# Transposes of x and x1 by VectorE and DMA in a four-layer graph attention kernel

## The chip, the cores and the metric

The kernel runs on one core of one Trainium2 chip. The core has five engines with queues of their own: TensorE (PE; its weight loads are shown as PEld), VectorE (DVE), ScalarE (ACT), GpSimd (POOL) and SyncE (SP), which here issues nearly all DMAs. The metric is the device time of the core in microseconds, the median of several runs; lower is better.

## The reference

16 samples x of 1024 nodes and 128 features pass through three transformer layers whose attention is masked by one adjacency matrix, and then through a graph attention layer:

```python
# layers 0 to 2, 8 heads of 16
scores = einsum('bnhd,bmhd->bhnm', h @ Wq, h @ Wk) / sqrt(16)
attn = softmax(where(adj == 0, -inf, scores))
x = layer_norm(h + (einsum('bhnm,bmhd->bnhd', attn, h @ Wv) @ Wo + bo), ln1_g, ln1_b)
x = layer_norm(x + relu(x @ W1 + b1) @ W2 + b2, ln2_g, ln2_b)
# layer 3
h = x @ W
e = leaky_relu((h @ a_src)[:, :, None] + (h @ a_dst)[:, None, :], 0.2)
out = layer_norm(softmax(where(adj == 0, -inf, e)) @ h + x, ln_gamma, ln_beta)
```

## The kernel before, in words

The work is cut into 48 **blocks**, one per sample and layer, in the order of `blocks` (line 655): four samples go through layer 0, then the same four through layers 1 and 2, then the next four. A block has 32 **steps**: two groups of four heads (g), two query halves (qh) and eight key tiles (kt). In a step (`score_step`, line 415) PE computes the scores of two pairs of heads, each into one of three PSUM buffers `s`; then each 128x1024 tile is masked and passed through exp in one of two ways. On DVE, a mask of zero or a large negative number is added while the tile is read from PSUM (L433), and ACT takes exp in place (L445). On POOL, ACT takes exp straight from PSUM (L430) and POOL multiplies by a mask of ones and zeros (L431). The second pair always goes through DVE; the first goes through POOL except in the steps named by `BOTH_ON_DVE`. Four steps later (`AHEAD`) `av_step` (line 447) multiplies by the values on PE and accumulates in `acc`, so PE, in its order, reaches the value matmul of a step behind the scores of the fourth step after it.

All other work is cut into **pieces**, at most one of them put behind a step by `piece` (line 691), in the order of a list of chains. Pieces of the kinds `proj` and `post` have a due step in the table `AT`; those of the last layer have a gap to the piece ahead of them. A chain that is due but stands behind another waits for a later step. For a block m:

- `proj_tasks(m)` (line 357) runs during block m-1: `t0` transposes x by halves on PE against an identity (`transpose_half`, line 281, instructions L286) and ACT copies it out of PSUM (L289, or L291 with the scale and shift of the norm before it); `split` projects to queries and keys and splits them into a high and a low part (L385 on ACT, L386 on DVE); `v` projects the values. Then `stack` (line 401) lays the parts out over partitions by 16 DMAs of 128 KB per head group (L408), the first group at step 21, the second at step 1 of the block itself.
- `post_tasks` (line 469) runs during block m+1: `gather` transposes the attention output on DVE (L477), `out_proj` projects it, DVE adds x (L329) and takes statistics (L322, L324), POOL normalises (`normalise`, L337 to L341), `x1t` transposes x1 on PE as above, POOL applies scale and shift (`scale_shift`, L345, L346), and `ffn1` and `ffn2` follow; after `ffn2` POOL normalises again, half by half.
- `last_tasks` (line 541) computes the last layer of a sample behind its third `post`: transposes, node values, rows g and h spread by 16 small DMAs, then four times `edges` and `aggregate`, and `end`, which stores the result.

The order of PE and ACT in the loop is as written; that of DVE, POOL and SP is settled by the scheduler when the kernel is built.[...]

Of the kernel before, what the change touches and what calls it, by code (L numbers as in the profile page):

```python
# [18 lines left out]
P = 128  # L19
# [4 lines left out]
SLOT = 32  # L24
# [9 lines left out]
AT = {"proj": (3, 6, 9, 11, 14, 17, 19, 20), "post": (12, 22, 23, 25, 26, 27, 28, 30, 32, 40, 41)}  # L34
AT_END = {3: (12, 21, 22, 24, 25, 26, 27, 28, 30, 31), 2: (8, 9, 13, 14, 15, 16, 17, 18, 20, 21)}
AHEAD = 4
BOTH_ON_DVE = (2, 5, 7)
TILES = {"w": 10, "x": LANES + 1, "last": 2}
# [77 lines left out]
def fast_path(ctx: ExitStack, tc: tile.TileContext, a: dict, out: bass.AP, flag):  # L116
# [32 lines left out]

    def load_x(b):  # L150
        t = work.tile([P, NT, D], F32, tag="x", name="x", bufs=TILES["x"])
        nc.sync.dma_start(t, x_dram[b].rearrange("(t p) d -> p t d", p=P))
        return t
# [115 lines left out]

    v_bufs = []  # L270
# [10 lines left out]
    def transpose_half(name, src, h, gain=None, bias=None):  # L281

        dst = half_tile(name)
        ps = bank()
        for t in range(4):
            nc.tensor.transpose(ps[:, t * P:(t + 1) * P], src[:, 4 * h + t, :], identf)  # L286
        with soon():
            if gain is None:
                nc.scalar.copy(dst, ps)  # L289
            else:  # L290
                nc.scalar.activation(dst, ps, AF.Identity, scale=gain, bias=bias)  # L291
        return dst

    def by_columns(dst, lhsT, rhs, start=True, stop=True):

        for j in range(0, P, SLOT):
            nc.tensor.matmul(dst[j:j + SLOT, :], lhsT[:, j:j + SLOT], rhs, start=start, stop=stop)  # L297
# [7 lines left out]
    def project(lhs, rhs, h, out):  # L305

        ps = bank()
        for t in range(4):
            for f in range(len(lhs)):
                by_columns(ps[:, t * P:(t + 1) * P], lhs[f][:, t * P:(t + 1) * P], rhs[f],  # L310
                           start=(f == 0), stop=(f == len(lhs) - 1))
# [45 lines left out]
    def proj_tasks(m):  # L357
        b, l = blocks[m]
        w = W[l]
        s = {}  # L360

        def t0(h):
            def run():
                x = state["x", b]
                if l == 0:
                    s["xT", h] = transpose_half("xT", x, h)
                    if h == 1:
                        nc.gpsimd.tensor_add(x, x, rows(w["bo"]))
                else:

                    s["xT", h] = transpose_half("xT", x, h, W[l - 1]["ln2_gc"], W[l - 1]["ln2_bc"])
                    if h == 1:
                        scale_shift(x, W[l - 1]["ln2_g"], w["bo"])
            return run

        def split(n, h):
            def run():
# [5 lines left out]
                by_columns(ps, w[n], s["xT", h])  # L383
                with soon():
                    nc.scalar.copy(hi[:, c], ps)  # L385
                    nc.vector.tensor_sub(lo[:, c], ps, hi[:, c].bitcast(F32))  # L386
            return run

        def v(h):
# [4 lines left out]
            return lambda: project([s["xT", h]], [w["Wv"]], h, out)  # L394

        pieces = [t0(0), t0(1), split("Wk", 0), split("Wk", 1), split("Wq", 0), split("Wq", 1), v(0), v(1)]
        return [(2 if n in (3, 4, 5, 6) else 1, f, {0: "+w", 1: "+w", 6: "-w", 7: "-w"}.get(n, "")) for n, f in enumerate(pieces)]
# [17 lines left out]
    def score_step(step):  # L415
# [3 lines left out]
        for pp in range(2):  # L419
# [7 lines left out]
            on_pool = pp == 0 and kt not in BOTH_ON_DVE  # L427
# [4 lines left out]
            else:  # L432
                behind["dve"] = nc.vector.tensor_add(ev, psv, m).ins  # L433
                masked.append((2 * step_no[0] + pp + (kt not in BOTH_ON_DVE), ev))
# [34 lines left out]
    def post_tasks(b, l):  # L469
# [20 lines left out]
        def x1t(h, alone=False):  # L490
            def run():
                x1 = s["n1"][0]
                s["x1T", h] = transpose_half("x1T", x1, h, w["ln1_gc"], w["ln1_bc"])
                if alone:
                    scale_shift(x1[:, 4 * h:4 * h + 4, :], w["ln1_g"], w["b2"])
                elif h == 1:
# [3 lines left out]
        def ffn1(f, h):  # L500
            def run():
                s["h", f, h] = half_tile("hT")
                ps = bank()
                by_columns(ps, w["W1"][:, f * P:(f + 1) * P], s["x1T", h])
# [4 lines left out]
        def ffn2(h):  # L509
            def run():  # L510
# [4 lines left out]
                normalise(s["n2"], slice(4 * h, 4 * h + 4))  # L515
# [7 lines left out]
        together = [(5, both, "+w +w"), (1, out_proj(0), "-w"), (1, out_proj(1), "-w"), (5, x1t(0), "+w"), (1, x1t(1), "+w")]  # L523
        for h in range(2):
            together += [(1, ffn1(0, h), "+w"), (1, ffn1(1, h), "+w -w")]
        together += [(1, ffn2(0), "-w -w"), (1, ffn2(1), "-w -w")]
        alone = [[(1, gather(h), "+w"), (1, out_proj(h), "-w"), (3, x1t(h, True), "+w"), (1, ffn1(0, h), "+w"),
                  (1, ffn1(1, h), "+w -w"), (1, ffn2(h), "-w -w")] for h in range(2)]
# [12 lines left out]
    def last_tasks(b):  # L541
# [3 lines left out]
        def xt(h):  # L545
            def run():
# [6 lines left out]
                s["xT", h] = transpose_half("xT", state["x", b], h, w["ln2_gc"], w["ln2_bc"])  # L553
# [44 lines left out]
        def edges(u):  # L598
            def run():
                e = s["e", u] = e_tile().rearrange("p j (c q) -> p (j c) q", q=256)  # L600
                for c in range(2):

                    ps = slot()
                    for i in range(2):
                        for r in range(2):
# [3 lines left out]
                                             g_rows[row, u * 256:(u + 1) * 256], start=True, stop=True)  # L609
                    nc.vector.scalar_tensor_tensor(e[:, c:NT:2, :], ps.rearrange("p (j q) -> p j q", q=256), 1.0,  # L610
                                                   mask01[:, c:NT:2, u * 256:(u + 1) * 256], op0=OP.max, op1=OP.mult)
            return run

        def aggregate(u):
            def run():
                e, ps = s["e", u], bank()
                for i in range(2):
                    for t in range(NT):
                        by_columns(ps[:, i * (D + 1):(i + 1) * (D + 1)], e[:, t, i * P:(i + 1) * P],
# [14 lines left out]
        def end():  # L634
            y = s["n"][0]
            for h in range(2):
                scale_shift(y[:, 4 * h:4 * h + 4, :], wl["ln_gamma"], wl["ln_beta"])
                queue = nc.scalar if h and b == B - 1 else nc.sync
                queue.dma_start(out[b].rearrange("(t p) d -> p t d", p=P)[:, 4 * h:4 * h + 4], y[:, 4 * h:4 * h + 4, :])
# [62 lines left out]
    with tc.manual_schedule(engines={mybir.EngineType.PE, mybir.EngineType.Activation, mybir.EngineType.DVE,  # L702
                                     mybir.EngineType.SP}):
        load_rows(range(4))
        put(proj_tasks(0), ("proj", 0))
# [21 lines left out]
    def av_due(n):  # L727

        for item in [w for w in waiting if w[2] <= n]:
# [24 lines left out]
            elif g == G - 1 and qh == 1:  # L754
                post = post_tasks(b, l)[0]
# [296 lines left out]
```

## Time and profile before

| | |
|---|---|
| median of 3 runs | 3985.54 us (3984.45 to 3985.72) |
| profiled execution | 3983.09 us |
| its span, first to last instruction | 3981.2 us |
| mean granted clock of TensorE | 0.987 |
| PE busy | 3758.5 us (94%) |
| DVE busy | 3408.3 us (86%) |
| ACT busy | 3392.8 us (85%) |
| POOL busy | 3331.4 us (84%) |
| share of the 16 DMA engines, SP's queue | 22.5% |

Durations below are those of the profiled execution, in us unless marked ns. An L number is a line of the kernel. Neighbouring instructions of DVE and ACT overlap by some 0.1 us, so that busy time is less than the count times the mean[...].

### The profile page before, as it was taken

How to read it: one execution, taken by the hardware profiler on the slowest of the kernel's cores; microseconds unless marked ns; L12 is line 12 of the kernel's file. 1: busy time of each engine (PE TensorE's matmuls, PEld its weight loads, DVE VectorE, ACT ScalarE, POOL GpSimd, SP SyncE). 2: the span in 40 equal slices, each digit the busy share in tenths (PEclk: the TensorE clock that was granted, in tenths of full speed). 3: DMA queues.
4: the chain of work that ended last, by engine and by line, in shares of the span. 5: the costliest groups of instructions: out<-in, count | busy, mean ns of one | idle time of the engine just before them, and what ended most of it. 6: DMA issues, size and time to landing. Idle time of an engine off the chain costs nothing.

```text
span 3981.2 us, 107823 instructions
## 1 busy us (share of the span) xinstructions
PE 3758.5 (94%) x44501; PEld 1558.5 (39%) x44501; DVE 3408.3 (86%) x5326; ACT 3392.8 (85%) x3961; POOL 3331.4 (84%) x3010
## 2 busy tenths in 40 slices
PE   7999999999999999999999999999999999999996
PEld 2333333344443333334444333333444433333345
DVE  7888988988888988988888898888888898898874
ACT  7999999977779999997777999999777799999860
POOL 4788888987789888988778888888877898898875
PEclk8999999999999999999999999999999999999998
DMA  6222222112222222222222222221222212222200
GB/s 163 65 65 53 55 65 63 46 48 65 56 58 57 65 65 54 54 65 55 55 55 55 65 53 56 65 64 45 55 55 55 71 46 62 65 51 58 66 8 20
DMA packets 124465, 233.13 MB, mean 59 GB/s; under 512 B 34624, under 2 KB 73792, under 8 KB 123968
## 3 DMA queue, kind: packets, MB, share of 16 engines
q1 hardware_dynamic: 123056, 225.74, 22.5%
q8 instruction: 354, 5.80, 0.6%
q14 instruction: 143, 1.17, 0.1%
q10 hardware_dynamic: 912, 0.42, 0.0%
HBM read 15.54 MB, written 8.39 MB: 6 GB/s over the span
## 4 chain that ended last, share of the span: by engine, by line
PE 61%; DVE 22%; POOL 9%; ACT 4%; issue 3%; SPq 0%; DMA 0%; DVEq 0%; ACTq 0%; POOLq 0%
PE acc L450 23%; PE t L297 19%; PE s L423 16%; DVE e L433 13%; POOL e L431 3%; POOL x L341 2%; PE t L286 2%; DVE lo L386 2%; DVE st L322 2%; ACT e L445 2%; ACT e L430 2%; DVE tt L461 1%; POOL mv L339 1%; PE s L297 1%; POOL x L345 1%
## 5 line engine op out<-in xcount | busy, mean ns | idle before, releaser
L433 DVE TENSOR_TENSOR e<-s,mask_add 128x1024 f32<-128x1024 f32 x2112 | 2493.6, 1213 | 344.6 <-PE s L423 263.7
L445 ACT ACTIVATE e<-e 128x1024 f32<-128x1024 f32 x2112 | 2203.4, 1060 | 206.1 <-DVE e L433 187.9
L431 POOL TENSOR_TENSOR e<-e,mask 128x1024 f32<-128x1024 f32 x960 | 1933.5, 2026 | 419.0 <-ACT e L430 419.0
L450 PE MATMUL acc<-e,v 128*17 128x512 f32 x12288 | 1627.8, 601 | 73.3 <-DVE tt L461 47.8
L423 PE MATMUL s<-Wq,Wk 64*128 64x512 f32 x6144 | 1185.0, 456 | 58.1 <-DVE e L433 41.3
L430 ACT ACTIVATE e<-s 128x1024 f32<-128x1024 f32 x960 | 980.8, 1022 | 227.5 <-PE s L423 226.5
L423 PEld LDWEIGHTS s<-Wq,Wk 64*128 64x128 f32 x6144 | 501.2, 185 | 1027.9 <-DVE e L433 417.1
L450 PEld LDWEIGHTS acc<-e,v 128*17 128x17 f32 x12288 | 208.6, 95 | 582.1 <-issue 452.0
L341 POOL TENSOR_SCALAR x<-x,mv 128x128 f32<-128x128 f32 x896 | 389.1, 447 | 23.5
L345 POOL TENSOR_TENSOR x<-x,ln_g 128x1024 f32<-128x1024 f32 (+1 forms) x97 | 229.5, 2367 | 25.1 <-PE t L286 22.6
L339 POOL TENSOR_TENSOR mv<-mv,half_neg 128x4 f32<-128x4 f32 x224 | 232.4, 1038 | 18.6
L297 PE MATMUL t<-hd,e 128*32 128x129 f32 x7040 | 208.2, 275 | 1.2
L329 DVE TENSOR_TENSOR x<-t,x 128x512 f32<-128x512 f32 x191 | 130.8, 685 | 86.9 <-PE t L297 86.9
L297 PEld LDWEIGHTS t<-hd,e 128*32 128x32 f32 x7040 | 194.6, 110 | 16.0 <-issue 5.0
L322 DVE BATCH_NORM_STATS2 st<-x 128x6 f32<-128x128 f32 x896 | 197.3, 280 | 3.3
L297 PE MATMUL t<-x1T,W 128*32 128x512 f32 x1520 | 198.0, 592 | 0.0
L297 PEld LDWEIGHTS t<-W,hT 128*32 128x32 f32 x6080 | 170.0, 110 | 58.5 <-issue 45.5
L297 PE MATMUL t<-W,hT 128*32 128x128 f32 x6080 | 183.4, 273 | 0.2 <-DVE x L625 0.2
L286 PE MATMUL t<-identf,x 128*128 128x128 f32 x872 | 151.0, 289 | 34.0 <-DVE lo L386 15.4
L286 PEld LDWEIGHTS t<-identf,x 128*128 128x128 f32 x872 | 92.9, 141 | 230.2 <-issue 108.3
L337 POOL TENSOR_SCALAR mv<-mv 128x4 f32<-128x4 f32 x224 | 53.0, 236 | 124.6 <-DVE mv L324 98.8
L610 DVE SCALAR_TENSOR_TENSOR e<-s,mask 128x1024 f32<-128x1024 f32 x128 | 150.3, 1214 | 5.9 <-PE s L607 5.0
(118 smaller groups left out, 2573.9 us busy)
## 6 DMA issues: line engine op xcount, KB each, us to landing
Wk<-hi SPq DMA_DIRECT2D x384, 128.0 KB
Wk<-lo SPq DMA_DIRECT2D x384, 128.0 KB
Wq<-hi SPq DMA_DIRECT2D x384, 128.0 KB
Wq<-lo SPq DMA_DIRECT2D x384, 128.0 KB
x<-in_x_dram SPq DMA_DIRECT2D x16, 512.0 KB
out_dram<-x SPq DMA_DIRECT2D x31, 256.0 KB
ai<-in_adj_dram SPq DMA_DIRECT2D x8, 512.0 KB
g_rows<-parts SPq DMA_DIRECT2D x124, 4.0 KB
```

The lines of the kernel that those rows point to most:

```text
L286: nc.tensor.transpose(ps[:, t * P:(t + 1) * P], src[:, 4 * h + t, :], identf)
L297: nc.tensor.matmul(dst[j:j + SLOT, :], lhsT[:, j:j + SLOT], rhs, start=start, stop=stop)
L322: nc.vector.bn_stats(st[:, t, :], z[:, t, :])
L339: nc.gpsimd.tensor_tensor(v, v, half_neg[:, ts], OP.pow)
L341: nc.gpsimd.tensor_scalar(z[:, t, :], z[:, t, :], mv[:, t, 0:1], mv[:, t, 1:2], op0=OP.add, op1=OP.mult)
L345: nc.gpsimd.tensor_mul(z, z, rows(gain, n))
L423: nc.tensor.matmul(ps[:, r * 512:(r + 1) * 512], k[64 * r:64 * r + 64, kt * P:(kt + 1) * P], q[64 * r:64 * r + 64, q0:q0 + 512], start=Tru ...
L430: nc.scalar.activation(ev, psv, AF.Exp, scale=HD ** -0.5)
L431: behind["pool"] = nc.gpsimd.tensor_mul(ev, ev, m).ins
L433: behind["dve"] = nc.vector.tensor_add(ev, psv, m).ins
L445: nc.scalar.activation(ev, ev, AF.Exp, scale=HD ** -0.5)
L450: nc.tensor.matmul(acc[j * SLOT:j * SLOT + HD + 1, :], v_bufs[m % 2][:, kt, 2 * j + g, :], e[:, j, :], start=first, stop=last)
```

## The change

1. **x and x1 are transposed without PE.** `transpose_by_dma`: two DVE instructions transpose a sample's tile in 32x32 blocks into a buffer `xb` (one buffer), and 16 DMAs on SP, of 32 KB each, carry the blocks to their partitions in `xT` or `x1T`. For this a sample's tokens are laid out in another order (`tokens`), so x is loaded by eight DMAs and the result stored by eight, and the last layer reads its mask and edge rows in strided form: four DVE instructions of 256 columns for one of 1024. PE still transposes x of the first block, x1 of the last two blocks and the input of the last layer.
2. **The call.** x for block m+2 is transposed at step 25 of block m, if it is ready; x1 is one piece, called with the table's step 17 ahead of `ffn1` at 24. Before it was a piece per half.
3. **Norm scale and shift** are folded into W1, b1, Wq, Wk, Wv and bo once, at step 40 (`fold_norms`). Queries and keys then have a bias of their own from layer 1 on, added in the instructions of `split`.
4. **Tables.** The due steps of all pieces, the steps in which both tiles are masked on DVE (11 of 32, not 12), the first stack at step 23, eight buffers `w` instead of ten, two buffers `xt` of a whole sample.
5. After `ffn2` POOL normalises all eight tiles at once, not four and four.

```diff
-AT = {"proj": (3, 6, 9, 11, 14, 17, 19, 20), "post": (12, 22, 23, 25, 26, 27, 28, 30, 32, 40, 41)}
+AT = {"proj": (6, 9, 15, 17, 19, 21), "post": (11, 13, 17, 24, 26, 28, 30, 32, 34)}
+AT_FIRST = (12, 14, 16, 18, 20, 22)
+T_AT = 25
+STACK_AT = 23
-BOTH_ON_DVE = (2, 5, 7)
-TILES = {"w": 10, "x": LANES + 1, "last": 2}
+BOTH_ON_DVE = (5, 7, 14, 16, 20, 22, 24, 26, 28, 30, 31)
+TILES = {"w": 8, "x": LANES + 1, "last": 2}
...
+    def tokens(v):
+
+        return v.rearrange("(h j t e) d -> j e h t d", h=2, j=4, t=4)
...
-        nc.sync.dma_start(t, x_dram[b].rearrange("(t p) d -> p t d", p=P))
+        for j in range(4):
+            queue = nc.scalar if b == 0 and j % 2 else nc.sync
+            for h in range(2):
+                queue.dma_start(t[j * SLOT:(j + 1) * SLOT, 4 * h:4 * h + 4], tokens(x_dram[b])[j][:, h])
...
+    def fold_norms():
+
+        cols = bank()
+        for l in range(L):
...
+                nc.tensor.matmul(cols[:, 8 * l + i:8 * l + i + 1], lhsT, rhs, start=True, stop=True)
+            nc.vector.tensor_add(W[l]["b1"], W[l]["b1"], cols[:, 8 * l:8 * l + NF])
+            nc.vector.tensor_scalar(W[l]["W1"], W[l]["W1"], W[l]["ln1_gc"], None, op0=OP.mult)
...
+    def transpose_by_dma(dst, src):
+
+        xb = work.tile([P, 4, 2, P], F32, tag="xb", name="xb", bufs=1)
+        for h in range(2):
+            nc.vector.transpose(xb[:, :, h, :].rearrange("p k (t e) -> p t k e", e=SLOT),
+                                src[:, 4 * h:4 * h + 4, :].rearrange("p t (k e) -> p t k e", e=SLOT))
+        for j in range(4):
+            for k in range(4):
+                nc.sync.dma_start(dst[k * SLOT:(k + 1) * SLOT, :, j * P:(j + 1) * P], xb[j * SLOT:(j + 1) * SLOT, k])
...
+                        b = w["b" + n]
+                        nc.scalar.activation(hi[:, c], ps, AF.Identity, scale=1.0, bias=b)
+                        nc.vector.scalar_tensor_tensor(lo[:, c], ps, b, hi[:, c].bitcast(F32), op0=OP.add,
+                                                       op1=OP.subtract)
...
-            on_pool = pp == 0 and kt not in BOTH_ON_DVE
+            both = now[0] % (4 * NT) in BOTH_ON_DVE
+            on_pool = pp == 0 and not both
...
-                s["x1T", h] = transpose_half("x1T", x1, h, w["ln1_gc"], w["ln1_bc"])
+                if h != 1:
+                    s["x1T"] = xt_tile("x1T")
+                if h is None:
+                    transpose_by_dma(s["x1T"], x1)
+                else:
+                    transpose_half(s["x1T"][:, h], x1, h)
...
-                normalise(s["n2"], slice(4 * h, 4 * h + 4))
+                if alone:
+                    normalise(s["n2"], slice(4 * h, 4 * h + 4))
+                elif h == 1:
+                    normalise(s["n2"], slice(0, NT))
...
-        together = [(5, both, "+w +w"), (1, out_proj(0), "-w"), (1, out_proj(1), "-w"), (5, x1t(0), "+w"), (1, x1t(1), "+w")]
+        together = [(5, both, "+w +w"), (1, out_proj(0), "-w"), (1, out_proj(1), "-w")]
+        together += [(5, x1t(0), ""), (1, x1t(1), "")] if quick else [(5, x1t(None), "")]
...
-                    nc.vector.scalar_tensor_tensor(e[:, c:NT:2, :], ps.rearrange("p (j q) -> p j q", q=256), 1.0,
-                                                   mask01[:, c:NT:2, u * 256:(u + 1) * 256], op0=OP.max, op1=OP.mult)
+                    for i in range(4):
+                        nc.vector.scalar_tensor_tensor(e[:, c + 2 * i, :], ps[:, i * 256:(i + 1) * 256], 1.0,
+                                                       queries(mask01[:, c + 2 * i, half]), op0=OP.max, op1=OP.mult)
...
-                queue.dma_start(out[b].rearrange("(t p) d -> p t d", p=P)[:, 4 * h:4 * h + 4], y[:, 4 * h:4 * h + 4, :])
+                for j in range(4):
+                    queue.dma_start(tokens(out[b])[j][:, h], y[j * SLOT:(j + 1) * SLOT, 4 * h:4 * h + 4, :])
...
+                    if at == (2 if m == 0 else 0) and ("xT", m + 1) not in state:
+                        need(source(m + 1))
+                        transpose_x(m + 1)
+                    if at == T_AT and m + 2 < len(blocks) and source(m + 2) in done:
+                        transpose_x(m + 2)
                     if at == (6 if m == 0 else 0):
-                        need(("post",) + (blocks[m + 1][0], blocks[m + 1][1] - 1) if blocks[m + 1][1] else
-                             ("fetch", blocks[m + 1][0]))
-                        put(proj_tasks(m + 1), ("proj", m + 1), first=True)
-                    if at == (24 if m == 0 else 21):
+                        put(proj_tasks(m + 1), ("proj", m + 1), first=True, table=AT_FIRST if m == 0 else None)
+                    if at == (24 if m == 0 else STACK_AT):
```

## The prediction

> **What bounds the kernel now.** I read the page first, then the stages, then the chain of one stage, then the order in which the changed kernel issues its instructions (it can be built without being run). A block is one sample in one layer: 32 steps, each with one query half and one key tile. The page's chain of work that ended last:
>
> ```profile
> PE 61%; DVE 22%; POOL 9%; ACT 4%; issue 3%; SPq 0%; DMA 0%; DVEq 0%; ACTq 0%; POOLq 0%
> PE acc L450 23%; PE t L297 19%; PE s L423 16%; DVE e L433 13%; POOL e L431 3%; POOL x L341 2%; PE t L286 2%; DVE lo L386 2%; DVE st L322 2%; ACT e L445 2%; ACT e L430 2%; DVE tt L461 1%; POOL mv L339 1%; PE s L297 1%; POOL x L345 1%
> ```
>
> PE leads, but the transposes to be removed (L286) are 2% of it, and the chain keeps changing engine. The ends of the blocks (every fourth L461 on DVE) show two kinds: some thirty plain blocks of 73.15 us each, and three groups of late ones (one of 80 us, then four of 92 to 99) in which the last layer of earlier samples is worked in. Busy time of one of each (columns: stage, length, then PE, PEld, DVE, ACT, POOL busy):
>
> ```profile
> 1304.40:1377.55 73.15, 70.69 (x722) 25.94 (x724) 65.14 (x98) 69.27 (x79) 64.63 (x57) 1.00 0.23 57
> 2016.70:2115.70 99.00, 91.87 (x1337) 44.50 (x1337) 81.53 (x141) 73.40 (x92) 78.69 (x76) 0.98 0.21 55
> ```
>
> In the plain block ACT is busy 95%; POOL's 57 instructions lie about 0.08 apart, so it has some 69 of 73 too; DVE has 65. Four engines are level. In the late block PE alone is near full. Rows of the kinds that the change touches (columns as on the page):
>
> ```profile
> L433 DVE TENSOR_TENSOR e<-s,mask_add 128x1024 f32<-128x1024 f32 x2112 | 2493.6, 1213 | 344.6 <-PE s L423 263.7 <-ACT e L445 56.4 <-POOL e L431 8.3
> L431 POOL TENSOR_TENSOR e<-e,mask 128x1024 f32<-128x1024 f32 x960 | 1933.5, 2026 | 419.0 <-ACT e L430 419.0
> L291 ACT ACTIVATE x1T<-t,ln_bc,ln_gc 128x512 f32<-128x512 f32 x95 | 73.3, 771 | 3.9 <-PE t L286 3.9
> L477 DVE STREAM_TRANSPOSE aT<-A 128x512 f32<-128x512 f32 x96 | 62.4, 687 | 2.9 <-POOL A L464 2.9
> ```
>
> The chain of work inside a plain block gives the pieces of PE (start, length):
>
> ```profile
> 1308.63 0.98 PE acc L450 x8
> 1309.61 0.59 PE t L286 x4
> 1310.20 0.69 PE s L423 x4
> ...
> 1316.92 0.90 PE t L297 x8
> ```
>
> So a step costs PE 1.65, a transposed half 0.6, a projection 0.87. And normalising half of a tile on POOL takes 3.5 from its first to its last instruction:
>
> ```profile
> 1374.86 0.24 POOL mv L337
> 1375.10 0.07 issue
> 1375.16 0.24 POOL mv L338
> 1375.40 0.07 issue
> 1375.47 1.05 POOL mv L339
> 1376.52 0.10 issue
> 1376.62 1.31 POOL x L341 x3
> ```
>
> The timeline of SP's queue shows one small DMA issue after another at 0.62:
>
> ```profile
> 1413.25 0.59 SPq L408 DMA_DIRECT2D Wk<-hi  x1
> 1413.89 0.59 SPq L408 DMA_DIRECT2D Wk<-lo  x1
> ```
>
> At the head, the last piece that the first scores need is issued until 17.33 and they start at 19.66: 2.3 to land.
>
> [...]
>
> **The change, part by part.**
>
> *Loads of a plain block.* PE loses four transposed halves: 4 x 0.6 = 2.4. ACT loses their four copies, about 0.68 net each since neighbours overlap by 0.1, and pays 4 x 0.12 for hi with a bias (a 697 ns form for a 583 ns one): 69.3 to 67.0. DVE gains four transposes at 0.63 net and loses one mask addition in 44 (1.15 net): 65.1 to 66.5. The transposes read and write in a four-dimensional pattern that no row shows; 0.69 if that is free, up to 1.4 if it doubles; I take 0.69. POOL gains one mask product (2.0), and loses one power (1.04) and two small ones (0.5) by normalising eight columns at once; if the wide power costs double, nothing is saved. POOL stays near 69.5. The biased lo is one DVE instruction as before. By loads alone a block could fall to some 71.
>
> *The waits of a plain block.* The order decides. Masks move: of steps 0 to 13 twelve now multiply on POOL, and normalising all of x comes there too. From the first exponential of the block POOL owes 11 x 2.0 + 5.8 (eight columns: 0.5 + 1.04 + 8 x 0.447 + gaps) + 1.2 (A, twice) before the first half of x1 is normalised, 3.5 more: 32.5. DVE's transpose of that half is ordered right after step 13's addition, and waits; behind it on DVE are the additions for steps 14 to 17, which PE's score buffers wait for. DVE then has 0.7 + 10.0 of work in order until the second half is transposed. Then 16 x 0.62 of issue and 2.3 to land: 12.2. Then PE, at step 24, takes the first FFN piece, 7 steps and 3 more pieces (15.0), and the next block's first exponential (1.4). The ring is 32.5 + 0.7 + 10.0 + 12.2 + 16.4 = 71.8; with DVE's pace in steps 24 to 31, 13 additions and 2.2 of other work behind the transposes (17.1), it is 73.5. I take 72.6: -0.5 x 30 = -15. Bounds: -2 (loads) and +2 (doubled transposes and power).
>
> *The late blocks.* Pieces of earlier samples take turns one per step. In the order of the changed kernel out_proj's halves come at steps 20 and 22 in six blocks (the second and third of 92 to 99 us in each group), x1's transpose is called at 23, and FFN1 stands on PE at 24, since its table says 24. Before, PE transposed at 27 and 29 and FFN1 followed at once, for 0.6 + 0.78. Now, from the second out_proj's end: addition and statistics 2.0, waiting for the additions of step 22 ahead of it, normalising 3.5, transpose 0.7, DMAs 12.2: 18.4, while PE has two steps, 3.3. DVE also waited for the first half, 4 us, which holds PE's scores. PE idle: about 15 + 4. It can't run past the waiting matmul, and DVE's next transpose waits for the same DMAs (xb is single). Against that: 2.4 less work and some 4 of the 7.1 idle that the block has now. Net +13 each, 78. The first late block of each group (second out_proj at 20): two steps and a projection more cover, +9, three of them: 27. The block before it has its 16 row DMAs ahead of x1's on SP (10 us), but x1 is ready early: +2, three: 6. The last of a group saves 2, three: -6.
>
> *Head.* Block 1's transpose puts 16 DMAs (10 us) between the two stacks of block 0; step 8 needs the second at about 53.5 and gets it near 57.5 to 62: +6. The row biases stand behind weights and transposes on SP; POOL, at step 20, waits some 5 more: +5. Folding: 22 small DVE instructions at about 0.2 ahead of step 40's additions, part of it in idle time, +3. Tail: x and out in quarters, +1 of issue; the last two blocks keep their transposes on PE.
>
> Edges: 512 of 256 columns for 128 of 1024; by the 416 ns row of that width +0.27 per four, 35 us of DVE in all, hidden where PE leads; if not, 2 per sample.
>
> Sum: -15 + 78 + 27 + 6 - 6 + 15 = +105. The profiled execution took 3983.09 (span 3981.2), the median is 3985.54: **4090**.
>
> **The rivals.** *Loads win (faster):* if POOL starts the block early enough and DVE never waits, plain blocks take 71.0, -2.1 x 30 = -63; with late stalls of 3 (x1T landing within the present idle), 9 x 3 + 15 = 42, 3964. For it: ACT and PE fall by 3%. Against: PE's fixed place at step 24. It decides once the late stall is under 5, or plain blocks are under 69.7. *The DMA path is slow:* if 64 pieces of 512 B cost 1.2 per issue, x1T comes 10 later everywhere, 30 x 8 + 9 x 10 = 330 more: 4420. SP's 0.43 to 0.64 for other shapes speak against. *DVE becomes the bound:* transposes of 1.3: 4 x 0.6 x 46 = +110, 4200. *Nothing is seen:* plain gains of -3.5 a block, from POOL's lighter second half, cancel it: 3985.
>
> **How the numbers follow.** Mine 0.72, loads 0.11, slow DMA 0.06, DVE 0.08, nothing 0.03. My late stall may be 8 to 20 (9 x 6 = 54 either way) and the plain block off by 1.5 (45): 4020 to 4160, to which the range adds part of the DVE case: 4005 to 4190. A difference under 0.2% can't be told from none here. Faster 0.11, same 0.03, slower 0.86.
>
> **What would show it.** PE waiting 10 to 16 us before FFN1 for a DMA x1T<-xb in nine late blocks, which then take 102 to 112 us; in plain blocks DVE's transpose waiting 3 to 4 for POOL's normalising, and ends 72 to 74 apart; the transpose near 690 ns, its issue near 0.6. Late blocks under 99 or plain ones under 71 would make me wrong.

## The result and the profile after

The changed kernel took 4606.04 us (median of four runs, 4601.70 to 4608.39) where the kernel before took 3984.99 on the same chip: 1.156 times as long, interval 1.154 to 1.158. I had forecast 4090. The direction was right; of the 621 us lost I had 105.

The page of the kernel after, its first lines and the granted TensorE clock by slices (digits are tenths of full speed):

```profile
span 4604.4 us, 109009 instructions
PE 3885.7 (84%) x43793; PEld 1511.0 (33%) x43793; DVE 3489.8 (76%) x5868; ACT 3293.4 (72%) x3777; POOL 3387.8 (74%) x2917
PEclk7999999999889999999888999999999899999998
```

TensorE runs 708 matmuls fewer than before (44,501), and yet is busy longer (3758.5 before). The clock dips to 0.8 three times, at the three groups of late blocks. Here is the first result to understand: next to nothing was added to TensorE, and its work takes 127 us more. The mean granted clock is 0.922, where it was 0.987. These traces have TensorE at 1.00 or at 0.50 and at nothing between, so that is some 718 us at half speed for 104 before (4604.4 x 0.078 x 2 and 3981.2 x 0.013 x 2).

The chain of work that ended last is of no use for this kernel: its view ends in the general path's branch behind the last block (three pieces on POOL, less than 2 us) and follows nothing back. So I went by blocks, read as before from every fourth transposition of acc. The same two views as before, for a plain and a late block (columns: stage, length, then PE, PEld, DVE, ACT, POOL busy, granted clock, DMA share, GB/s):

```profile
463.77:545.86 82.09, 71.91 (x704) 24.66 (x704) 66.43 (x100) 67.28 (x75) 65.84 (x55) 0.96 0.28 69
1217.27:1341.55 124.28, 95.95 (x1333) 43.44 (x1325) 84.77 (x169) 70.78 (x87) 79.81 (x74) 0.89 0.21 53
```

Three loads are as forecast: DVE 66.43 (66.5), ACT 67.28 (67.0), POOL 65.84 and 55 gaps of 0.08, 70.2 in all (69.5). TensorE's 71.91 stands against 68.3 (70.69 less 2.4), with a lower clock. No engine is near 82. The loss is waits, and a clock of 0.96 and 0.89. Rows of the page, for the kinds that the change touches:

```profile
L494 DVE TENSOR_TENSOR e<-s,mask_add 128x1024 f32<-128x1024 f32 x2064 | 2427.0, 1207 | 346.2 <-PE s L483 208.0
L492 POOL TENSOR_TENSOR e<-e,mask 128x1024 f32<-128x1024 f32 x1008 | 2031.8, 2025 | 812.8 <-ACT e L491 807.0
L338 DVE STREAM_TRANSPOSE xb<-x 128x512 f32<-128x512 f32 x184 | 127.9, 702 | 308.4 <-POOL x L397 199.4
L395 POOL TENSOR_TENSOR mv<-mv,half_neg 128x4 f32<-128x4 f32 (+1 forms) x177 | 213.3, 1205 | 14.7
L538 DVE STREAM_TRANSPOSE aT<-A 128x512 f32<-128x512 f32 x96 | 66.5, 701 | 123.1 <-POOL A L525 123.1
```

The new transposes take 702 ns, no more than the plain ones (701). They are 184, two for each of 92 tiles: 47 of x and 45 of x1, so TensorE keeps x1 of the last three blocks, not two. But VectorE now stands 199.4 us at xb for a normalising of GpSimd (POOL), and 123.1 us at aT, where the kernel before had 2.9. GpSimd in turn stands 807 for exponentials (419 before). Each engine waits for the next.

Where the 623 us of span went, by kinds of block (us; there are 29 plain blocks and three groups of five late ones, counted from the block that took 80 before):

| kernel | blocks 0 and 1 | plain, mean | late group, sum of five | last two | rest |
|---|---|---|---|---|---|
| before | 183.7 | 73.16 | 463.5 | 188.8 | 96.6 |
| after | 218.3 | 82.61 | 563.4 | 198.3 | 101.8 |
| lost in all | 35 | 274 | 300 | 10 | 5 |

**One plain block.** VectorE's timeline, its two long waits (start, length, engine, line, ..., idle before and its releaser):

```profile
473.03 0.71 DVE L538 STREAM_TRANSPOSE aT<-A 128x512 f32<-128x512 f32 x1 [3.32 <-POOL A L525]
...
492.50 0.71 DVE L338 STREAM_TRANSPOSE xb<-x 128x512 f32<-128x512 f32 x1 [3.27 <-POOL x L397]
```

GpSimd's timeline says what is late at the first:

```profile
464.55 0.25 POOL L393 TENSOR_SCALAR mv<-mv 128x8 f32<-128x8 f32 x1
464.87 0.25 POOL L394 TENSOR_SCALAR mv<-mv 128x8 f32<-128x8 f32 x1
465.21 1.67 POOL L395 TENSOR_TENSOR mv<-mv,half_neg 128x8 f32<-128x8 f32 x1
466.99 3.46 POOL L397 TENSOR_SCALAR x<-x,mv 128x128 f32<-128x128 f32 x8
470.40 2.02 POOL L492 TENSOR_TENSOR e<-e,mask 128x1024 f32<-128x1024 f32 x1
472.37 0.63 POOL L525 TENSOR_TENSOR A<-tt,recs 128x256 f32<-128x256 f32 x1
```

All eight tiles of x are normalised (5.9 us) ahead of A. Nobody needs x before the transposing of the next layer, but VectorE's aT needs A, and behind aT in VectorE's order stand the mask additions: the first of them started at 473.77, after the 3.32 for A and aT itself, though TensorE had ended the last scores before its own stall by 471.93. In the kernel before, only four tiles stood ahead of A, and aT came 6.4 us after A was written (GpSimd's and VectorE's timelines of before):

```profile
1303.48 1.74 POOL L341 TENSOR_SCALAR x<-x,mv 128x128 f32<-128x128 f32 x4
1307.16 0.62 POOL L464 TENSOR_TENSOR A<-tt,recs 128x256 f32<-128x256 f32 x1
1314.17 1.29 DVE L477 STREAM_TRANSPOSE aT<-A 128x512 f32<-128x512 f32 x2
```

There the second half of FFN2 was due at step 40 and its four tiles were normalised behind A; the new table has it at 34, and all eight are normalised once it is done. TensorE's timeline of the changed kernel shows both stalls:

```profile
471.44 0.49 PE L483 MATMUL s<-Wq,Wk 64*128 64x512 f32 x2
475.03 0.70 PE L483 MATMUL s<-Wq,Wk 64*128 64x512 f32 x2 [3.10 <-DVE e L494]
475.66 1.91 PE L511 MATMUL acc<-e,v 128*17 128x512 f32 x8
477.50 1.21 PE L483 MATMUL s<-Wq,Wk 64*128 64x512 f32 x4
478.64 1.05 PE L511 MATMUL acc<-e,v 128*17 128x512 f32 x8
```

It stops for a free score buffer, 3.10 here and 3.99 at 495. And then look at the lengths: eight matmuls of acc take 1.91 right after the stall and 1.05 three us later. The granted clock of the same stretch (columns as in the stages above; the clock is third from the end):

```profile
466.00:472.00 6.00, 5.93 (x70) 2.17 (x66) 3.49 (x3) 5.03 (x6) 5.89 (x10) 1.00 0.00 1
475.00:479.00 4.00, 3.97 (x18) 0.98 (x22) 2.41 (x3) 3.50 (x4) 1.88 (x1) 0.57 0.02 4
479.00:485.00 6.00, 6.00 (x74) 2.36 (x68) 4.69 (x5) 5.77 (x7) 4.86 (x4) 1.00 0.01 1
495.00:499.00 4.00, 4.00 (x20) 0.96 (x22) 3.22 (x10) 3.14 (x4) 2.67 (x6) 0.58 0.00 0
```

After each stall the clock is 0.57 or 0.58 for four us, which costs 4 x 0.43 = 1.7 more. The block's account, beside the plain block of before at 1304.40: idle time of TensorE went from 2.46 to 10.18, +7.7 (the two stalls alone are 7.1); its busy time from 70.69 to 71.91, +1.2, though it has 2.4 less to do. Together these are the 8.94 by which this block is longer. It is not the worst: by the clock in the trace the mean plain block is at half speed for 9.5 us, this one for 6.8.

**One late block.** TensorE's longest wait there, and the stages that follow it:

```profile
1299.43 1.94 PE L348 MATMUL t<-x1T,W 128*32 128x512 f32 x8 [15.01 <-DMA x1T<-xb]
```

```profile
1275.00:1285.00 10.00, 5.74 (x24) 1.09 (x22) 5.82 (x13) 3.97 (x4) 5.54 (x10) 0.66 0.59 145
1285.00:1295.00 10.00, 0.00 (x0) 0.00 (x0) 2.95 (x3) 1.06 (x1) 6.33 (x6) 0.63 0.13 33
1295.00:1305.00 10.00, 5.57 (x24) 1.32 (x24) 2.53 (x3) 3.48 (x4) 4.06 (x2) 0.52 0.15 36
```

The stall at FFN1 that I forecast (10 to 16) is there, 15.01, but two more are ahead of it in the same block (3.96 for a product of GpSimd, 3.68 for VectorE standing at xb), and the clock is at half behind each, by the trace's clock for 3.4, 5.2 and 5.2 us.

And SP's queue, for x1 of the plain block:

```profile
504.99 10.33 SPq L342 DMA_DIRECT2D x1T<-xb  x15
```

0.69 per DMA; I had taken 0.62.

### The profile page after: what moved, and what is told of

The parts are those of the page before. It is cut to its first block, busy times and chain, and to the rows that moved or that the text cites. A ratio compares the mean times of both kernels' runs of the same rounds, so it can differ in the third digit from the quotient of the medians.

```text
span 4604.4 us, 109009 instructions
## 1 busy us (share of the span) xinstructions
PE 3885.7 (84%) x43793; PEld 1511.0 (33%) x43793; DVE 3489.8 (76%) x5868; ACT 3293.4 (72%) x3777; POOL 3387.8 (74%) x2917
## 5 line engine op out<-in xcount | busy, mean ns | idle before, releaser
L494 DVE TENSOR_TENSOR e<-s,mask_add 128x1024 f32<-128x1024 f32 x2064 | 2427.0, 1207 | 346.2 <-PE s L483 208.0
L492 POOL TENSOR_TENSOR e<-e,mask 128x1024 f32<-128x1024 f32 x1008 | 2031.8, 2025 | 812.8 <-ACT e L491 807.0
L506 ACT ACTIVATE e<-e 128x1024 f32<-128x1024 f32 x2064 | 2142.9, 1058 | 640.9 <-DVE e L494 626.7
L511 PE MATMUL acc<-e,v 128*17 128x512 f32 x12288 | 1720.3, 633 | 119.1 <-DVE tt L522 76.5
L483 PE MATMUL s<-Wq,Wk 64*128 64x512 f32 x6144 | 1268.3, 476 | 359.7 <-DVE e L494 293.6
L338 DVE STREAM_TRANSPOSE xb<-x 128x512 f32<-128x512 f32 x184 | 127.9, 702 | 308.4 <-POOL x L397 199.4
L395 POOL TENSOR_TENSOR mv<-mv,half_neg 128x4 f32<-128x4 f32 (+1 forms) x177 | 213.3, 1205 | 14.7
L572 ACT ACTIVATE hT<-t,b 128x512 f32<-128x512 f32 x190 | 128.9, 678 | 129.2 <-PE t L348 129.0
L687 DVE SCALAR_TENSOR_TENSOR e<-s,mask 128x256 f32<-128x256 f32 x512 | 175.1, 412 | 8.5 <-PE s L683 8.2
L538 DVE STREAM_TRANSPOSE aT<-A 128x512 f32<-128x512 f32 x96 | 66.5, 701 | 123.1 <-POOL A L525 123.1
```

Of the source, the lines that this page charges most:

```text
L395: nc.gpsimd.tensor_tensor(v, v, half_neg[:, ts], OP.pow)
L483: nc.tensor.matmul(ps[:, r * 512:(r + 1) * 512], k[64 * r:64 * r + 64, kt * P:(kt + 1) * P], q[64 * r:64 * r + 64, q0:q0 + 512], start=Tru ...
L492: behind["pool"] = nc.gpsimd.tensor_mul(ev, ev, m).ins
L506: nc.scalar.activation(ev, ev, AF.Exp, scale=HD ** -0.5)
L511: nc.tensor.matmul(acc[j * SLOT:j * SLOT + HD + 1, :], v_bufs[m % 2][:, kt, 2 * j + g, :], e[:, j, :], start=first, stop=last)
L687: nc.vector.scalar_tensor_tensor(e[:, c + 2 * i, :], ps[:, i * 256:(i + 1) * 256], 1.0, queries(mask01[:, c + 2 * i, half]), op0=OP.max, o ...
```

## The experiments

Each is a single execution with its profile (four of the changed kernel lay within 7 us); the kernel before took 3981.8 to 3983.7 beside them. The table has the time, and from the trace the mean plain block and the sum of a late group:

| run | time | plain | late group |
|---|---|---|---|
| before | 3984.99 | 73.16 | 463.5 |
| after | 4606.04 | 82.61 | 563.4 |
| e1 old list of masks | 4434.40 | 80.12 | 533.2 |
| e2 x1 by TensorE, 17 and 18 | 4425.20 | 82.47 | 505.1 |
| e3 x by TensorE | 4712.63 | 84.90 | 579.7 |
| e4 before, new list | 4101.74 | 75.32 | 478.0 |
| e7 x1 by TensorE, 22 and 23 | 4374.11 | 80.88 | 504.6 |
| e8 FFN1 7 steps after x1 | 4489.67 | 82.79 | 524.0 |
| e9 aT behind the additions | 4473.87 | 79.01 | 553.8 |
| e10 aT and xb behind them | 4294.58 | 75.13 | 534.9 |
| e11 e10 and e8 | 4268.03 | 75.33 | 526.3 |
| e12 both by TensorE | 4344.10 | 79.19 | 513.2 |
| e13 e10, x1 by TensorE in late blocks | 4175.36 | 75.02 | 496.6 |
| e14 e13, old list | 4240.02 | 79.63 | 472.4 |

### First round: which part of the change costs it

e1, the old list of mask products:

```diff
-            both = now[0] % (4 * NT) in BOTH_ON_DVE
+            both = kt in (2, 5, 7)
```

> The changed kernel with the old choice of mask products (key tiles 2, 5 and 7 of every eight on VectorE) in place of the new list by step; all else stays. Theory Order (VectorE's in-order transposes wait for GpSimd, which the new list loads in steps 0 to 13): GpSimd is 3 to 4 products lighter ahead of x1's normalising, so plain blocks fall from 82 to 77 or 78 and the time from 4606 to 4430 to 4480; late blocks keep their wait for x1T. Theory List (the new list itself paces the block, VectorE being full in steps 24 to 31): plain blocks fall to 74 or less, the time to about 4330. Theory Path (the transposing by VectorE and DMA costs it all): nothing moves, 4580 to 4630.

4434.40: in Order's range by its total, but plain blocks stayed at 80, not 77 to 78, and the late groups gave the rest (30 each). In the block that I read the wait at x1's half is gone, as Order has it, and the one at aT is not (3.19); TensorE still stalls once for over 2 us, 2.97.

e2, x1 transposed by TensorE:

```diff
-AT = {"proj": (6, 9, 15, 17, 19, 21), "post": (11, 13, 17, 24, 26, 28, 30, 32, 34)}
+AT = {"proj": (6, 9, 15, 17, 19, 21), "post": (11, 13, 17, 18, 24, 26, 28, 30, 32, 34)}
-                post = post_tasks(b, l, len(blocks) - m in AT_END)[0]
+                post = post_tasks(b, l, True)[0]
```

> The changed kernel with x1 transposed by TensorE (two halves, at steps 17 and 18, FFN1 still from 24 on); x stays with VectorE and DMAs. Theory Order: the wait of VectorE for half a normalised x1 goes (3.3 a block[...]), plain blocks 77 to 78; late blocks lose their 16 us for x1T and fall from 124 to about 100: 4606 - 30 x 4.5 - 9 x 20 = about 4290. Theory List: only the late blocks gain, 4606 - 9 x 16 = about 4460. Theory Path: plain blocks back to 74 or 75, 4190.

4425.20. Late blocks gained 58 a group, plain ones nothing (82.47). Order, as I had put it, is refuted for the plain blocks. TensorE's timeline there shows two stalls still, 2.90 for a mask addition and 2.93 for a product of GpSimd, and two shorter ones (1.16 and 0.85) at the transposes, which at 17 and 18 may be too early; e7 puts them later.

e3, x transposed by TensorE:

```diff
-    def transpose_x(m, by_dma=True):
+    def transpose_x(m, by_dma=False):
```

> The changed kernel with x transposed by TensorE where the transposing was called (step 25, or step 0); x1 stays with VectorE and DMAs. Theory Order: x's transposing waits only 1.1 in a plain block, so plain blocks stay at 81 to 83, late ones at 114 to 125: 4580 to 4640. Theory Path: the single buffer xb and SP's queue are freed, plain blocks fall by 3 or more: below 4520.

4712.63, slower than either theory. Freeing xb and SP's queue of x gains nothing, so this form of Path falls. Both stalls of the plain block are still there (3.12 and 4.02), and behind each TensorE is at half speed for 6.8 us, where the changed kernel's block has 3.4; why the run is 107 slower was not taken apart further.

e4, the new list in the kernel before:

```diff
-BOTH_ON_DVE = (2, 5, 7)
+BOTH_ON_DVE = (5, 7, 14, 16, 20, 22, 24, 26, 28, 30, 31)
-            on_pool = pp == 0 and kt not in BOTH_ON_DVE
+            on_pool = pp == 0 and now[0] % (4 * NT) not in BOTH_ON_DVE
```

> The kernel before with the new list of steps whose masks are both added by VectorE; nothing else. Theory Order: the list alone costs 1 to 3 a block, since nothing of VectorE's waits for GpSimd's normalising there: 4030 to 4130. Theory List: plain blocks go to 80 or more, 4200 to 4300. Theory Path: no change, 3970 to 4000.

4101.74, in Order's range: 2.2 us a plain block. List falls as the main cause; alone it costs 118 in all.

### Second round: the two waits of VectorE

e5, aT let in later:

```diff
-        together = [(5, both, "+w +w"), (1, out_proj(0), "-w"), (1, out_proj(1), "-w")]
+        together = [(8, both, "+w +w"), (1, out_proj(0), "-w"), (1, out_proj(1), "-w")]
```

> The changed kernel with the transposing of A (aT, and out_proj behind it) let in 8 steps after its block's end instead of 5, so that VectorE's aT stands behind later mask additions; nothing else. Theory First stall (aT waits 3.3 a block, because the normalising of all eight tiles of x now comes ahead of A on GpSimd[...]): plain blocks fall from 82 to 77 or 78, 4606 - 36 x 4.5 = about 4440. Theory Ring (GpSimd's work up to x1's normalising, and the wait there, set the length whatever happens before): aT's wait goes and x1's grows, plain blocks stay at 81 to 83, 4580 to 4620.

4608.56, and the wait that was to go is still there (waits of e5: who for whom, total, times, longest):

```profile
DVE aT L538 <- POOL A L525: 124.7, 34, 7.3
```

The experiment did not do what it said. VectorE's order in the attention loop isn't that of the code; a planner sets it, and it came out the same instruction for instruction, as did those of TensorE, ScalarE and GpSimd. The run repeats the changed kernel and decides nothing, but it told me what to change (e9).

e6, the normalising of x in halves:

```diff
-        together += [(1, ffn2(0), "-w -w"), (1, ffn2(1), "-w -w")]
+        together += [(1, ffn2(0, True), "-w -w"), (1, ffn2(1, True), "-w -w")]
```

> The changed kernel with the normalising of x after FFN2 in two halves, each behind its own half as in the kernel before, instead of eight tiles at once; nothing else. Theory First stall: A comes some 3 us earlier for aT, plain blocks fall by 2 to 3, 4606 - 36 x 2.5 = about 4515. Theory Ring: GpSimd has the same work or 0.8 more, plain blocks stay within 1 of 82: 4580 to 4640.

4605.30, as Ring had it. A's place didn't move, though (GpSimd's and VectorE's timelines of e6):

```profile
472.68 0.63 POOL L525 TENSOR_TENSOR A<-tt,recs 128x256 f32<-128x256 f32 x1
...
473.34 0.71 DVE L538 STREAM_TRANSPOSE aT<-A 128x512 f32<-128x512 f32 x1 [3.50 <-POOL A L525]
```

Both halves are still normalised ahead of A. That eight columns go in one power (1.67, two of 1.04 in halves) is thus no cause; that the normalising stands ahead of A may be. No run put the second half of FFN2 back to step 40.

e7, x1 by TensorE near where the kernel before had it (23 and 25 in its table):

```diff
-AT = {"proj": (6, 9, 15, 17, 19, 21), "post": (11, 13, 17, 24, 26, 28, 30, 32, 34)}
+AT = {"proj": (6, 9, 15, 17, 19, 21), "post": (11, 13, 22, 23, 25, 26, 28, 30, 32, 34)}
-                post = post_tasks(b, l, len(blocks) - m in AT_END)[0]
+                post = post_tasks(b, l, True)[0]
```

> The changed kernel with x1 transposed by TensorE at steps 22 and 23, where the kernel before had it, and the first FFN1 at 25; x stays with VectorE and DMAs. With the transposing at 17 and 18 plain blocks stayed at 82 to 83, TensorE itself waiting for x1 then. Theory Second stall (x1's transposing waits wherever it comes before GpSimd is through, at 22 it comes after): plain blocks 78, late 98 to 106, 4606 - 32 x 4 - 9 x 19 = about 4310. Theory Ring: plain blocks stay above 81, 4400 to 4440.

4374.11, between the two by its total; the plain blocks, 80.9, are nearer Ring's 81 than 78. With x1's transposing off VectorE the stalls sat elsewhere. TensorE's timeline of e7, one plain block:

```profile
462.88 0.79 PE L483 MATMUL s<-Wq,Wk 64*128 64x512 f32 x2 [2.89 <-DVE e L494]
463.60 1.91 PE L511 MATMUL acc<-e,v 128*17 128x512 f32 x8
...
492.31 1.25 PE L511 MATMUL acc<-e,v 128*17 128x512 f32 x8 [2.94 <-POOL e L492]
493.32 1.95 PE L348 MATMUL t<-xT,Wq 128*32 128x512 f32 x8
```

At the first, VectorE's xb for the next x waits 3.03 for the same normalising of eight tiles (it has come ahead of aT); at the second TensorE waits for GpSimd's products, which the new list heaps into steps 8 to 13. Again each of them is followed by matmuls at half speed. So this plain block of e7 has two stalls with their price, as the changed kernel has, for other reasons.

e8, FFN1 at least 7 steps behind x1's transposing:

```diff
-        return now[0] >= (chain["due"] + gap if at is None else at)
+        return now[0] >= (chain["due"] + gap if at is None else max(at, chain["due"] + gap))
-        together += [(5, x1t(0), ""), (1, x1t(1), "")] if quick else [(5, x1t(None), "")]
+        together += [(5, x1t(0), ""), (1, x1t(1), "")] if quick else [(4, x1t(None), "")]
-            together += [(1, ffn1(0, h), "+w"), (1, ffn1(1, h), "+w")]
+            together += [(7 - 6 * h, ffn1(0, h), "+w"), (1, ffn1(1, h), "+w")]
```

> The changed kernel with the first FFN1 at least 7 steps behind the transposing of x1 by DMAs, where the table alone had it at 24; in plain blocks nothing moves. Theory Late wait (in late blocks TensorE stands 15 us at FFN1 for x1T): the nine blocks lose 10 or more each, 102 to 115 instead of 114 to 125: 4606 - 9 x 10 = about 4515. Theory Given back (the FFN that comes later holds the next block's start or out_proj): below 30 in all, 4580 to 4610.

4489.67, 116 gained: the first four blocks of a group fell from 103, 116, 124 and 125 to 94, 110, 92 and 102, and the fifth rose from 96 to 127. So Late wait is right on the cause, and of 70 us saved in a group 31 were given back.

### Third round: VectorE's order alone

e9 orders aT on VectorE behind the newest mask addition (issue_after names the instruction that it must follow), e10 does the same for both transposes into xb. No data, buffer, list or table changes. TensorE's and ScalarE's orders are those of the changed kernel, instruction for instruction; in GpSimd's a few move:

```diff
-                nc.vector.transpose(s["aT", h], att[:, h].rearrange("p k g d -> p (k g d)"))
+                with tc.issue_after(behind["dve"]) if late else nullcontext():
+                    nc.vector.transpose(s["aT", h], att[:, h].rearrange("p k g d -> p (k g d)"))
```

with the gap of 8 of e5, and for e10 besides:

```diff
-            nc.vector.transpose(xb[:, :, h, :].rearrange("p k (t e) -> p t k e", e=SLOT),
-                                src[:, 4 * h:4 * h + 4, :].rearrange("p t (k e) -> p t k e", e=SLOT))
+            with tc.issue_after(behind["dve"]):
+                nc.vector.transpose(xb[:, :, h, :].rearrange("p k (t e) -> p t k e", e=SLOT),
+                                    src[:, 4 * h:4 * h + 4, :].rearrange("p t (k e) -> p t k e", e=SLOT))
```

> The changed kernel with aT let in at 8 steps instead of 5, and ordered on VectorE right behind the newest mask addition at that step (the earlier run with 8 alone left VectorE's order as it was); nothing else. Theory Stalls (a wait of VectorE for GpSimd starves TensorE for over 3 us, and TensorE's clock is near half for 4 us after: 3.1 + 1.7 for aT, 4.0 + 1.7 for xb, together the loss of a plain block): plain blocks fall from 82 to 77, 4606 - 34 x 4.8 = about 4440. Theory Ring (GpSimd's queue sets the length): plain blocks stay at 80 to 82, above 4550.

> The same, and the transposes into xb also ordered on VectorE right behind the newest mask addition of the step where they are called (17 for x1, 25 or 0 for x); the transposing, the lists and tables stay. Theory Stalls: both stalls go, plain blocks 73 to 75, late blocks as before or some us longer since x1T starts later: 4606 - 34 x 8 = about 4330. Theory Ring: the stall only moves (TensorE waits for a product of GpSimd, as with x1 by TensorE, or at FFN1), plain blocks 78 to 81, 4450 to 4560.

4473.87 and 4294.58: plain blocks at 79.0, then 75.1, where the changed kernel has 82.6 and Ring had 80 to 82 and 78 to 81. The aT stall was worth 3.6 rather than the 4.8 that I expected, xb's 3.9. The plain block of e10 (stage, columns as above), and VectorE's aT in it:

```profile
438.80:513.91 75.11, 68.69 (x704) 24.01 (x704) 66.73 (x101) 66.70 (x75) 65.83 (x55) 1.00 0.32 76
```

```profile
455.68 1.26 DVE L540 STREAM_TRANSPOSE aT<-A 128x512 f32<-128x512 f32 x2
```

GpSimd's timeline of the same block, from the normalising on:

```profile
442.01 3.48 POOL L398 TENSOR_SCALAR x<-x,mv 128x128 f32<-128x128 f32 x8
445.45 2.04 POOL L493 TENSOR_TENSOR e<-e,mask 128x1024 f32<-128x1024 f32 x1
447.44 0.63 POOL L526 TENSOR_TENSOR A<-tt,recs 128x256 f32<-128x256 f32 x1
448.02 9.94 POOL L493 TENSOR_TENSOR e<-e,mask 128x1024 f32<-128x1024 f32 x5
457.92 0.63 POOL L526 TENSOR_TENSOR A<-tt,recs 128x256 f32<-128x256 f32 x1
```

In this stretch GpSimd has the same instructions in the same order as in the changed kernel, A behind eight normalised tiles (later in the block two products move ahead of a scaling). But the five products between the two A run without a gap, 9.94, where the changed kernel had 13.3 for them (472.94 to 486.27) with three waits for ScalarE. GpSimd wasn't too slow; it was starved by the engine that waited for it.

The clock is 1.00 again and TensorE is busy 68.69 instead of 71.91 with the same 704 matmuls: 3.2 us of a plain block were slow clock. aT waits for nothing; the whole of VectorE's wait there is 4.6 us in e10, 123.1 before that. Where VectorE's transposes stand in its order is thus worth 311 us. A plain block is still 2.0 longer than before, with 2 us less for TensorE to do; there TensorE waits 1.87 for aT and 0.96 for x1T, and no run took that rest apart.

e11 is e10 with the edit of e8:

> The same, and the first FFN1 at least 7 steps behind the transposing of x1. Theory Stalls: plain blocks 73 to 75, late ones as in the run with that edit alone (its gain was 116): about 4220. Theory Ring: plain blocks 78 to 81, 4350 to 4450.

4268.03, a gain of 27 where the edit alone had 116: the third and fourth block of a group fell by 25 and 16, and the fifth rose by 37, from the 85 that it had in e10. Its time lies between the two theories, its plain blocks (75.3) nearer Stalls.

e12, both transposed by TensorE, e7's and e3's edits together:

> The changed kernel with x and x1 both transposed by TensorE (x where it was called, x1 at 22 and 23): folding, list and tables stay, no DMA and no xb. Theory Stalls: aT still waits, and GpSimd's products in steps 8 to 13 are late, so plain blocks take 77 to 80 and late ones 97 to 107: 4250 to 4370. Theory Path (the transposing itself): plain blocks 73 to 75.5, 4000 to 4120.

4344.10, in the range of Stalls. This kernel has no transposing by DMA in its blocks at all, and its plain blocks take 79.2, 6.0 more than before. The stall at aT is there (waits of e12):

```profile
DVE aT L538 <- POOL A L525: 123.4, 34, 7.3
```

So the transposing itself is not what the change mainly pays for in plain blocks; the tables and orders that came with it are.

### Fourth round: what is left in the late blocks

e13 is e10 with x1 by TensorE in the late blocks alone:

```diff
+AT_LATE = (11, 13, 22, 23, 25, 26, 28, 30, 32, 34)
-                post = post_tasks(b, l, len(blocks) - m in AT_END)[0]
+                late = m % 12 in (9, 10, 11, 0, 1) and m > 1
+                post = post_tasks(b, l, late or len(blocks) - m in AT_END)[0]
-                put(post[1:], ("post", b, l), chain, table=AT_END.get(len(blocks) - m))
+                put(post[1:], ("post", b, l), chain, table=AT_END.get(len(blocks) - m) or (AT_LATE if late else None))
```

and e14 is e13 with e1's edit.

> VectorE's transposes ordered behind the mask additions, and x1 transposed by TensorE (at 22 and 23, FFN1 from 25) in the late blocks alone; plain blocks keep the transposing by DMAs. Theory x1T alone (the late blocks' loss is FFN1's wait for x1T and the slow clock after it): blocks that took 120 to 122 fall to 96 to 100, those of 107 to 95, time 4295 - 6 x 22 - 3 x 12 = about 4125. Theory Mixed (GpSimd behind with its products, and the tables, cost there too): they fall only to 104 to 109, time about 4190.

> The same with the old choice of mask products (key tiles 2, 5, 7 of every eight on VectorE). Theory: once nothing of VectorE's waits for GpSimd the new list costs what it cost the kernel before, 1 to 2.3 a block: plain blocks 73 to 74, 60 to 100 less than the run without. Rival: the new list suits the new order, VectorE being nearly full (67.4 of 74 with the old choice): no change or up to 50 more.

4175.36: the blocks that took 121 fell to 108 to 109, as Mixed had it, those of 107 to 96, as x1T alone had it; the total is nearer Mixed. 4240.02 for e14, 65 more, outside both ranges: the old list costs plain blocks 4.6 (79.63 for 75.02; with it they wait for x1T, 80.3 us in 30 times) and saves a late group 24 (472.4 for 496.6). With the old list the late groups are within 9 us of the kernel before. What the list costs thus depends on what stands around it: in plain blocks the new one loses 2.2 in the kernel before and 2.5 in the changed kernel (e1), and gains 4.6 here.

No kernel of these is faster than the one before.

## Why the prediction was wrong

**Loads of a plain block: right.** Those of DVE, ACT and POOL came within 0.7 us; TensorE's 68.3 came out as 68.69 only in e10, where its clock is whole. With the four-dimensional pattern a transpose took 702 ns, as I had taken it, and not 1.4 us; the plain ones took 701. The loads decided nothing.

**The waits of a plain block: this step failed.** I forecast a ring of 32.5 + 0.7 + 10.0 + 12.2 + 16.4 = 71.8, up to 73.5 with VectorE's pace (73.9 where 17.1 takes the place of 15.0), and took -15 for all of them. The same pieces in the trace, in the same order: from the first exponential (453.53) to the first half of x1 normalised (492.44) 38.9; from its transpose (492.50) to the end of the second half's (504.26) 11.8; until FFN1 on TensorE (517.01) 12.7; to the next first exponential (535.62) 18.6. That is 82.0. The middle terms held within 1.1 (10.7 and 12.2). The first term was 6.4 short. GpSimd stood 5.1 of that waiting for exponentials; another 1.1 is the first exponential itself, which my sum left out. The wide power took 0.63 more than the narrow one, which I had taken as equal, but the normalising of eight tiles as a whole took 5.85 for the 5.8 forecast. The last term was 2.2 over the 16.4.

Why GpSimd stood is the error proper. I had counted the normalising of eight tiles into GpSimd's sum, but did not ask who waits for what it was moved ahead of. A is behind it; aT waits for A; behind aT on VectorE are mask additions; TensorE waits for those, ScalarE for TensorE, GpSimd for ScalarE. I had named the second stall ("DVE's transpose of that half is ordered right after step 13's addition, and waits") and measured it at 3.27 now against 3 to 4 forecast, and then let the ring hide it. A ring's length is no cover: its terms contain the wait's consequences. e9 and e10 show it, since reordering these transposes, with TensorE's and ScalarE's orders as they were, takes 7.5 us off the block.

**The clock: missing altogether.** Both stalls of the plain block were followed by half speed, for 3.41 us each; e10 puts that at 3.2 in the block that I read, a third of its loss. My sum has no term for it: it prices a stall of TensorE at its length alone. By the traces half speed lasts 3.41 us or a multiple, and of stalls of 2.9 some are followed by it and some not, as the last section shows. In the kernel before, TensorE has nine waits of over 2 us in the whole run, all in the first 36 us or after 3830, and none in a plain block.

**The late blocks: right in mechanism, short in size.** I forecast +13 for each of six, 9 for each of three, 2 and -2 for the others: 35 a group, and it was 100. By the successive edits: VectorE's order 28 (e10), x1T by DMAs, with FFN1's wait and the slow clock behind it, 38 (e13 against e10), the new list 24 (e14 against e13), 9 left, which no run took apart. The x1T term was thus 38 against 35, and block by block 1.7, 11.7, 12.5, 12.6 and -0.5 against my 2, 9, 13, 13 and -2. That holds for this order of the edits: taken out of the changed kernel first (e2) the same step gains 58. The other two are VectorE's stalls, of which I had priced one, at 4, in six blocks, and the list, that I had costed as one mask addition in 44.

**Head.** +35 for +15. The forecast waits came: 6.43 for the second stack, 4.87 for the biases, 1.74 at the folding. Block 1 has the plain blocks' stall too (3.94 and its clock). And TensorE's clock is at half from 55.3 to 69.0, around the first two waits, and from 140.7 to 150.9, at the folding, where the kernel before has it whole from 48 on. That explains part of the rest; what remains was not tried.

**The rivals.** The slow DMA path would have given 4420, but an issue costs 0.69, not 1.2; VectorE as the bound, 4200, fails at 702 ns. The time landed beyond all of them for a reason that none had. Loads win needed VectorE not to wait, and the trace shows it waiting over 3 us twice a block; even with the order mended (e10) plain blocks take 75.1, not 71.0.

## What to carry to other kernels

When an instruction is moved forward on an engine that works in order, as VectorE does at aT here (3.32 for A, and the additions behind it), list what now stands behind it, and for each of those who waits, until the loop closes; a wait of 3 us on a side engine is not hidden because a longer ring exists. Price a stall of TensorE of about 3 us at its length and, by e2's stalls of 2.89 to 2.98, 0 to 3.4 more: 1.7 for each step of 3.41 us that the clock stays at half, and they had none, one or two. And before an edit is judged by a run, see that the engine's order really changed: two of these fourteen moved code and not the instruction that mattered.

## What the runs showed of the hardware that I had not expected

TensorE's clock is 0.50 or 1.00 in these traces. Each stretch at half speed between head and tail lasts a whole number of steps of 3.41 us, and the stretches of a run all begin on one grid of that step (110 stretches in the changed kernel). Where in a step a stall ends matters: the changed kernel has 35 of 3.92 to 4.04 that begin at full speed between head and tail; the 19 that ended 0.99 to 2.33 us into a step were followed by two steps of half speed, the 15 that ended 2.47 to 2.97 into it by one, and so was one at 0.78. Near 3 us the length doesn't decide it: e2 has 57 stalls of TensorE of 2.89 to 2.98 that begin at full speed: 20 were followed by no half speed, 27 by one step of it, 10 by two. Here are two of 2.93, both for a product of GpSimd, and what follows each (timeline, and the stages with the clock third from the end):

```profile
497.36 1.05 PE L511 MATMUL acc<-e,v 128*17 128x512 f32 x8 [2.93 <-POOL e L492]
579.18 1.91 PE L511 MATMUL acc<-e,v 128*17 128x512 f32 x8 [2.93 <-POOL e L492]
```

```profile
497.36:500.77 3.41, 3.41 (x28) 0.83 (x28) 0.72 (x1) 1.43 (x2) 3.12 (x7) 1.00 0.56 135
579.18:584.60 5.42, 5.42 (x24) 1.19 (x28) 0.54 (x1) 1.65 (x3) 5.13 (x8) 0.50 0.35 85
```

In the changed kernel all 93 stalls of 3.0 us and more that began at full speed, head and tail left out, were followed by half speed, 44 of them for one step and 39 for two. In e3 a stall of 3.12, which cost one step in the changed kernel (3.10), was followed by two:

```profile
476.10:482.90 6.80, 5.58 (x26) 1.48 (x30) 4.65 (x5) 4.88 (x5) 4.16 (x3) 0.50 0.00 1
```

Of the stall of 15.01, half speed began within it, at 1287.5, and ended 5.2 after it, at 1304.6: a stall five times as long left less slow work behind it than this one of 3.12.

GpSimd's power over 128x8 took 1.67 us and over 128x4 1.04: an estimate from these two is 0.16 per column and 0.41 at the start.
